# New durations in a kernel's own list schedule, an add moved ahead of a scaling, and a later row for a second recurrence

## The chip, the cores and the metric

The kernel runs on one core of a Trainium2 chip. The metric is the device time of one execution in microseconds (us), as the median of several runs; lower is better. A core has five engines that each work through their own instructions in order and wait for each other through semaphores: TensorE (PE: matmuls and transposes, results in PSUM), VectorE (DVE), ScalarE (ACT), GpSimd (POOL) and SyncE (SP), which here only issues DMAs. PSUM has eight banks of 512 floats a row. All data is float32; a float32 matmul stands in the trace as two passes.

## The reference

The input `x` has 2 sequences of 4096 tokens with 256 channels. Two sublayers are applied, each on a layer-normed input with a residual around it.

The first is a recurrence over all tokens, channel by channel:

```
r, k, v = three projections of mixes of a token and the one before it
out_t = (exp(b-p)*a + exp(k_t+u-p)*v_t) / (exp(b-p) + exp(k_t+u-p) + eps)
a, b  = a decayed running sum of exp(k)*v, and the log of that of exp(k)
y     = group_norm(sigmoid(r) * out) @ W_o.T
```

The second has two layers, each an attention over windows of 128 tokens that also sees the window before, and a gated feed-forward part:

```
h = shift_token(x);  q, k, v = split(h @ wqkv)          # 8 heads of 64
q, k = rotary(l2norm(q) * qs), rotary(l2norm(k) * ksc)
x = x + softmax(8 q k^T, masked to i-128 <= j <= i) v @ wo
h = layer_norm(shift_token(x)) @ w1 + b1;  a, g = split(h)
x = x + (a * gelu(g)) @ w2 + b2                          # 682 hidden channels
```

## The kernel before

**Tiling.** Tokens are taken in groups of 128, one window each: 2 sequences x 2 layers x 32 windows are 128 groups, numbered `n` from 0 to 127. Four groups make a block of 512 tokens, `k`. Blocks 0 to 7 are sequence 0 in layer 0, blocks 8 to 15 sequence 0 in layer 1, and blocks 16 to 31 the same for sequence 1. The recurrence of sequence 0 (`rec`, pieces of 512 tokens) runs first, that of sequence 1 (`rec2`, 16 pieces of 256 tokens) beside the attention and feed-forward work of sequence 0. Its tiles lie in one buffer, `arena`, so the profile names its work `arena` (the first one also borrows `hm`, `x`, `qk`, `sq`, `hT` and others).

**A group's attention.** For group `n`, `transpose_qk` turns queries and keys, `scores` makes the scores of eight heads in four PSUM banks, in one piece with the products of group `n-1`'s probabilities with its values (`values`). `softmax(n, g)`, g from 0 to 3, handles two heads of one bank: `copy_predicated` packs the two windows' scores into the 129 columns that a query can see, a minimum over them gives the shift `nmx`, ScalarE takes the exponentials into `pr` with their sums in `sums`, VectorE the reciprocal, and `scaled` multiplies `pr` by it. Column 0 of `pr` holds the weight of the last token of the window before, column 1 that of the first token of the own window; each later column holds a token of one of the two windows. `transpose_p(n, s)`, s = 0 or 1, takes four heads (g = 0, 1 or g = 2, 3): it adds column 0 of `pr` to column 1 (lines 1102 to 1104), then transposes columns 1 to 128 on TensorE; the value products take these with the own values `vt`, and a masked copy `pB`, into which the transposed column 0 goes as row 0, with `dv`, the older values less the own. The sum of columns 0 and 1 is what makes the two products add up to both weights. A group that opens a sequence (`lone(n)`) has no window before it and needs no add.

**What sets the order.** The program isn't issued as it is written. `Plan` (line 174) records every operation with what it depends on, and a row (`plan.at`, mostly `n`). `cost` (line 294) gives each operation a `step`, after which its engine is free for the next, and a `time`, after which its result is there, from constants of its kind and its number of elements. `order` (line 361) then walks a list schedule: on each engine it takes the operation that can start first, and among those that can start within 1 ns of it the one of the smallest row:

```
for s, g in cands:
    if s <= t0 + 1:
        key = g[0].at
        if best is None or key < best[0]:
            best = (key, s, g)
```

Operations marked "either" (copies, and the scalings `scaled`) go to whichever of VectorE and ScalarE could start them first. `lock` marks operations of VectorE and GpSimd that are taken not to overlap; `TURN` is what TensorE is taken to lose between matmuls of full size and those of half the rows or columns. PSUM banks are handed out in the same walk. `give` (line 487) emits the operations in order of their planned starts. On the chip, each engine follows that order and waits where the plan was wrong. All emitted instructions stand in the profile under the lines of `give`: L503, with L497 and L499 for `scaled` on VectorE and ScalarE.

**The second recurrence.** In the loop over `n` (line 1359 on), piece `c` of `rec2` is recorded at row `n + 0.5` of the group with `int(c * R_SLOTS / rec2.n) == n`, R_SLOTS being 54: its scans, and ahead of them load, norm, transposes and projections of piece `c + 1`. Rows only rank operations that are ready together.

Of the kernel before, what the change touches and what calls it, by code (L numbers as in the profile page):

```python
# [30 lines left out]
LN_EPS = 1e-5  # L31
NEG = -1e38
MASKED = -3e38
R_SLOTS = 54
AHEAD = 1

ARENA = (
# [18 lines left out]

SEM = 60
LOAD = 1283
TURN = {"row": 195, "col": 95, "full": 95}
SETS = {AF.Exp: 1, AF.Tanh: 1, AF.Gelu: 2, AF.Ln: 3}  # L60
QUADS = 4

# [111 lines left out]
class Plan:  # L174
# [119 lines left out]
    def cost(self, o):  # L294
# [6 lines left out]
        if o.eng == "tensor":  # L301
# [10 lines left out]
                o.step /= 2  # L312
            o.time = o.step + 150
        elif o.eng == "vector":
            if name == "tensor_tensor_reduce":
                d = 210 + 1.05 * n
            elif name == "tensor_tensor_scan":
                d, o.lock = 2.48 * n, True
            elif name in ("scalar_tensor_tensor", "tensor_tensor"):
                d, o.lock = 175 + 1.04 * n, wide > 1  # L320
            elif name in ("tensor_scalar", "tensor_copy") and not psum:
                d, o.lock = 230 + 0.45 * n, n > 64
            elif name == "bn_aggr":
                d = 180
            elif name == "reciprocal":
                d = 165 + 4 * n
            else:
                d = 150 + 1.04 * n
            o.step, o.time = max(d - 70, 60), d
        elif o.eng in ("scalar", "either"):  # L330
            d = 160 + 0.83 * n
            if name == "scaled":
                d = 40 + 1.4 * n
            if name == "activation":
                o.set = SETS.get(o.args[2])
                if "accum_out" in o.kw:
                    d += 320
                elif o.args[2] in (AF.Gelu, AF.Identity):
                    d = 40 + 1.4 * n
            o.step, o.time = d - 100, d  # L340
        elif o.eng == "gpsimd":
            if name == "tensor_tensor":
                d = 600 + 160 * n if ALU.pow in o.args else 150 + 2.25 * n
                o.lock = n > 64
            elif name == "tensor_scalar":
                d = 200 + 1.12 * n
                o.lock = n > 64
            else:
                d = 170 + 0.98 * n
                o.lock = n > 64  # L350
            o.step, o.time = d, d
        else:
            v = min(views, key=lambda v: v.shape[0] * v.idx.size)
            size = 4 * v.shape[0] * v.idx.size
            rows = max(v.shape[0] if v.shape[0] > 1 else v.shape[1] for v in views)
            ways = max(k for k in range(1, 17) if rows % k == 0)
            o.passes = size / 170 if ways == 16 else size / (25 * ways)
            o.step, o.time = 60, 2000 + o.passes


    def order(self):
# [47 lines left out]
        while todo:  # L409
# [23 lines left out]
            for o in g:  # L433
# [73 lines left out]
def kernel(ctx: ExitStack, tc: tile.TileContext, a: dict, out: bass.AP):  # L507
# [547 lines left out]
    def softmax(n, g):  # L1055
# [27 lines left out]
        for m in range(2):  # L1083
# [272 lines left out]
    for n in range(NN + 6):  # L1356
# [152 lines left out]
```

## Time and profile before

| what | us |
|---|---|
| median of 3 runs | 3045.44 |
| lowest and highest of them | 3045.35 and 3046.44 |
| the profiled execution, its own time | 3047.84 |
| its span in the trace | 3046.0 |
| TensorE: matmuls 128x512 with `wqkv` | 728.1 busy, 1536 passes of 598 ns |
| TensorE: matmuls 128x512 with `w1` (`hT`) | 646.7 busy, 1408 passes of 595 ns |
| VectorE: adds of `pr`, 128x4 | 61.5 busy, 248 of 248 ns |
| VectorE: scalings of `pr`, 128x129 (L497) | 84.9 busy, 274 of 336 ns |
| ScalarE: scalings of `pr`, 128x129 (L499) | 260.0 busy, 738 with the 128x128 ones, 398 ns each |
| ScalarE: exponentials into `pr` | 362.4 busy, 1024 of 365 ns |
| ScalarE: loads of its function tables | 146.3 busy, 114 of 1283 ns |

Busy time of an engine is the time in which an instruction of it is in flight; two that follow each other closely overlap. A "releaser" is the instruction whose semaphore ended a wait. The mean granted clock of TensorE is 0.994 of full speed.

### The profile page before, as it was taken

The page shows a single profiled execution, that of the slowest core. Times are in us where ns is not written, and L with a number is a line of the kernel's source. Part 1 is how long each engine was busy: PE and PEld are TensorE (multiplying, and loading weights), DVE is VectorE, ACT ScalarE, POOL GpSimd, SP SyncE. Part 2 cuts the span into 40 slices and gives each one's busy share as a digit, 9 for nine tenths or more (in the row PEclk, how much of TensorE's full clock was granted, in tenths as well). Part 3 has the DMA queues.
Part 4 walks back from the last instruction along what each step waited for, and adds up shares of the span by engine and source line. Part 5 has one row for each costly group of instructions (what it writes and reads, how often), then busy time and mean ns, then how long its engine had stood idle before and what let it go on. Part 6 is the DMA issues. An engine that isn't in the chain of part 4 may idle for free.

```text
span 3046.0 us, 47917 instructions
## 1 busy us (share of the span) xinstructions
PE 2977.8 (98%) x15500; PEld 1932.6 (63%) x15500; DVE 2513.2 (83%) x5487; ACT 1731.2 (57%) x4592; POOL 1434.7 (47%) x1705
## 2 busy tenths in 40 slices
PE   8979999999999999999999999999999999999998
PEld 3456566666666666666666666666666666666665
DVE  7889999989889898887787787878878787877774
ACT  6877665666556666655555455545545555555542
POOL 2227555445444545444455444444444554554541
PEclk9989999999999999999999999999999999999999
DMA  3222112111112121111112211112112111111110
GB/s 96 88 76 89 44 57 63 53 58 51 59 51 80 54 69 54 53 53 56 53 54 82 83 58 60 57 59 60 54 45 66 61 59 56 55 53 51 48 43 23
DMA packets 178163, 181.66 MB, mean 60 GB/s; under 512 B 27028, under 2 KB 147700, under 8 KB 177400
## 3 DMA queue, kind: packets, MB, share of 16 engines
q1 hardware_dynamic: 177912, 178.59, 19.0%
q8 instruction: 123, 2.02, 0.3%
q14 instruction: 128, 1.05, 0.1%
HBM read 78.38 MB, written 33.55 MB: 37 GB/s over the span
## 4 chain that ended last, share of the span: by engine, by line
PE 75%; DVE 13%; ACT 6%; issue 2%; POOL 2%; SPq 1%; DMA 1%; DVEq 0%; POOLq 0%; ACTq 0%
PE bank L503 75%; DVE arena L503 3%; ACT arena L503 2%; DVE sq L503 1%; DVE qk L503 1%; ACT L503 1%; DVE bank L503 1%; SPq L503 1%; DVE nmx L503 1%; DVE x L503 1%; ACT pr L499 1%; DVE pr L497 1%; DMA h<-x 1%; DVE hm L503 1%; POOL rs L503 1%
## 5 line engine op out<-in xcount | busy, mean ns | idle before, releaser
L503 PE MATMUL bank<-wqkv,xT 128*128 128x512 f32 x1536 | 728.1, 598 | 0.0
L503 PE MATMUL bank<-hT,w 128*128 128x512 f32 (+1 forms) x1408 | 646.7, 595 | 0.2 <-DVE hT L503 0.2
L503 POOL TENSOR_TENSOR t<-qk,tab 128x256 f32<-128x256 f32 x512 | 379.8, 762 | 502.5 <-DVE qk L503 293.8
L503 ACT ACTIVATE pr<-bank,nmx 128x129 f32<-128x129 f32 (+1 forms) x1024 | 362.4, 365 | 332.3 <-DVE nmx L503 331.8
L503 PEld LDWEIGHTS bank<-hT,w 128*128 128x128 f32 (+1 forms) x1408 | 257.6, 190 | 273.1 <-issue 256.4
L503 PEld LDWEIGHTS bank<-wqkv,xT 128*128 128x128 f32 x1536 | 269.1, 190 | 240.1 <-issue 230.4
L503 POOL TENSOR_TENSOR rn<-rn,mhalf 128x16 f32<-128x16 f32 x128 | 386.1, 3017 | 10.3
L503 PE MATMUL bank<-w,hm 128*128 128x256 f32 x1536 | 351.8, 379 | 0.0
L503 PEld LDWEIGHTS bank<-w,hm 128*128 128x128 f32 x1536 | 287.1, 190 | 51.1 <-issue 15.3
L499 ACT ACTIVATE pr<-pr,sums 128x129 f32<-128x129 f32 (+1 forms) x738 | 260.0, 398 | 40.6 <-DVE sums L503 38.0
L503 PE MATMUL bank<-kT,qT 64*128 64x256 f32 (+1 forms) x2048 | 252.4, 386 | 0.0
L503 PE MATMUL bank<-wo,oT 128*128 128x256 f32 x1024 | 248.0, 385 | 2.5 <-ACT oT L503 1.7
L503 PEld LDWEIGHTS bank<-wo,oT 128*128 128x128 f32 x1024 | 189.7, 190 | 74.7 <-issue 35.4
L503 DVE TENSOR_TENSOR pB<-bank,backs 128x512 f32<-128x512 f32 x248 | 169.3, 683 | 51.8 <-ACT pT L503 50.0
L503 PEld LDWEIGHTS bank<-kT,qT 64*128 64x128 f32 x2048 | 185.3, 186 | 39.0 <-issue 15.9
L503 PEld LDWEIGHTS bank<-mats,pr 128*128 128x128 f32 (+1 forms) x1148 | 130.8, 135 | 120.2 <-issue 40.3
L503 DVE COPY_PREDICATED bank<-packs,bank 128x254 f32<-128x254 int32 x496 | 186.0, 420 | 25.1 <-PE bank L503 24.9
L503 ACT ACTIVATION_READ_ACCUMULATOR pr<-bank,nmx 128x1 f32 x1024 | 206.7, 202 | 0.0
L503 PE MATMUL bank<-pT,vt 128*64 128x128 f32 x2048 | 203.6, 279 | 0.0
L503 PE MATMUL bank<-mats,pr 128*128 128x128 f32 (+1 forms) x1148 | 173.3, 275 | 22.1 <-DVE pr L503 18.8
L503 PE MATMUL bank<-arena,wold 128*128 128x256 f32 (+1 forms) x600 | 193.7, 447 | 0.4 <-DMA wold<-in_w_rkv_dram 0.4
L503 POOL TENSOR_TENSOR tab<-tab,qks 128x256 f32<-128x256 f32 x128 | 109.6, 857 | 177.2 <-DMA tab<-in_c_rot_dram 167.3
(148 smaller groups left out, 5440.6 us busy)
## 6 DMA issues: line engine op xcount, KB each, us to landing
vr<-vt SPq DMA_DIRECT2D x124, 224.0 KB
tab<-in_c_rot_dram SPq DMA_DIRECT2D x128, 128.0 KB
kT<-kT SPq DMA_DIRECT2D x64, 256.0 KB
z<-zd SPq DMA_DIRECT2D x16, 512.0 KB
x<-in_x_dram SPq DMA_DIRECT2D x16, 512.0 KB
x1d<-x SPq DMA_DIRECT2D x16, 512.0 KB
x<-x1d SPq DMA_DIRECT2D x16, 512.0 KB
h<-x SPq DMA_DIRECT2D x128, 64.0 KB
```

Source lines behind the costliest of these rows:

```text
L497: self.nc.vector.tensor_scalar(dst, src, scale, None, ALU.mult)
L499: self.nc.scalar.activation(dst, src, AF.Copy, scale=scale)
L503: getattr(getattr(self.nc, o.eng), name)(*args, **kw)
```

## The change

It has three parts. First, constants in `cost`, `order` and `TURN`, which say how long operations take: among them a ScalarE scaling of 129 columns goes from 40 + 1.4 x 129 to 305 + 0.76 x 129 ns, an exponential with its sum from 160 + 0.83 x 129 + 320 ns to 160 + 0.83 x 129 + 85 ns of engine time with another 200 ns to its result, a VectorE scaling from 230 + 0.45 x 129 to 155 + 0.98 x 129 ns, and the turn of TensorE to full size from 95 to 199 ns. The tail of a VectorE instruction that may overlap the next goes from 70 to 85 ns. Second, the add of `pr`'s columns 0 and 1 moves from `transpose_p`, after the scaling, to `softmax`, between reciprocal and scaling, where it takes two heads at a time. Third, pieces of `rec2` are recorded five groups later (NW is 4) and closer together (R_SLOTS 50 for 54).

```diff
-R_SLOTS = 54
+R_SLOTS = 50
...
-TURN = {"row": 195, "col": 95, "full": 95}
+TURN = {"row": 195, "col": 95, "full": 199}
...
         elif o.eng == "vector":
+            d = 150 + 1.04 * n
             if name == "tensor_tensor_reduce":
-                d = 210 + 1.05 * n
+                d = 240 + 1.04 * n
             elif name == "tensor_tensor_scan":
-                d, o.lock = 2.48 * n, True
-            elif name in ("scalar_tensor_tensor", "tensor_tensor"):
-                d, o.lock = 175 + 1.04 * n, wide > 1
-            elif name in ("tensor_scalar", "tensor_copy") and not psum:
+                d, o.lock = 203 + 2.1 * n, True
+            elif name == "scalar_tensor_tensor":
+                d, o.lock = 200 + 1.05 * n, wide > 1
+            elif name == "tensor_tensor":
+                o.lock = wide > 1
+            elif name == "tensor_scalar":
+                d, o.lock = 155 + (1.27 if psum else 0.98) * n, not psum and n > 64
+            elif name == "tensor_copy" and not psum:
                 d, o.lock = 230 + 0.45 * n, n > 64
...
-            o.step, o.time = max(d - 70, 60), d
+            o.step, o.time = max(d - 85, 60), d
+        elif o.eng in ("scalar", "either"):
+            d = (160 if psum else 195) + 0.83 * n
+            if name == "scaled":
+                d = 305 + 0.76 * n
+            elif name == "activation":
+                o.set = SETS.get(o.args[2])
+                if o.args[2] == AF.Identity:
+                    d = 365 + 0.87 * n
+                elif isinstance(o.kw.get("bias"), View):
+                    d += 85
+            o.step, o.time = d - 100, d
+            if "accum_out" in o.kw:
+                o.time = d + 200
...
-        elif o.eng in ("scalar", "either"):
-            d = 160 + 0.83 * n
-            if name == "scaled":
-                d = 40 + 1.4 * n
-            if name == "activation":
-                o.set = SETS.get(o.args[2])
-                if "accum_out" in o.kw:
-                    d += 320
-                elif o.args[2] in (AF.Gelu, AF.Identity):
-                    d = 40 + 1.4 * n
-            o.step, o.time = d - 100, d
...
-                    time = 150 + 1.04 * n if o.name == "copy" else 230 + 0.45 * n
-                    step = time - 70
+                    time = 150 + 1.04 * n if o.name == "copy" else 155 + 0.98 * n
+                    step = time - 85
...
         nc.vector.reciprocal(sums, sums)
+        if not lone(n):
...
+            p0 = prs[n][:, h0 : h0 + 3 : 2, :]
+            nc.vector.tensor_tensor(p0[:, :, 1], p0[:, :, 1], p0[:, :, 0], ALU.add)
         for m in range(2):
             ph = prs[n][:, h0 + 2 * m, off:]
             nc.either.scaled(ph, ph, sums[:, m : m + 1])
...
         pr = prs[n]
-        if not lone(n):
-            p0 = pr[:, 4 * s : 4 * s + 4, 1]
-            nc.vector.tensor_tensor(p0, p0, pr[:, 4 * s : 4 * s + 4, 0], ALU.add)
         ppt = bank([P, 4, W])
...
         for c in range(rec2.n):
-            if int(c * R_SLOTS / rec2.n) == n:
+            if NW + 1 + int(c * R_SLOTS / rec2.n) == n:
                 plan.at(n + 0.5)
```

GpSimd's constants change in the same way, by up to 30% (its power function on one element from 760 to 586 ns).

More of the change, by code (lines that the diff above doesn't have):

```diff
@@ L322, in cost @@
                 d, o.lock = 230 + 0.45 * n, n > 64
             elif name == "bn_aggr":
-                d = 180
+                d = 172
             elif name == "reciprocal":
-                d = 165 + 4 * n
-            else:
-                d = 150 + 1.04 * n
-            o.step, o.time = max(d - 70, 60), d
-        elif o.eng in ("scalar", "either"):
-            d = 160 + 0.83 * n
-            if name == "scaled":
-                d = 40 + 1.4 * n
-            if name == "activation":
-                o.set = SETS.get(o.args[2])
-                if "accum_out" in o.kw:
-                    d += 320
-                elif o.args[2] in (AF.Gelu, AF.Identity):
-                    d = 40 + 1.4 * n
-            o.step, o.time = d - 100, d
[L341 to L350, printed above, removed]
+                d = 147 + 4 * n
@@ new lines, in cost @@
+            o.step, o.time = max(d - 85, 60), d
[12 more added lines that the diff above has]
+                o.time = d + 200
+        elif o.eng == "gpsimd":
+            o.lock = n > 64
+            if name == "tensor_tensor":
+                d = 430 + 156 * n if ALU.pow in o.args else 140 + 2.22 * n
+            elif name == "tensor_scalar":
+                d = 230 + 1.12 * n
+            else:
+                d = (100 if name == "memset" else 187) + 0.98 * n
```

## The prediction

> **What bounds the kernel now.** I read the page's busy shares and chain first, then the windows by stage, then TensorE's waits, then one late transpose in the timeline.
>
> ```profile
> PE 2977.8 (98%) x15500; PEld 1932.6 (63%) x15500; DVE 2513.2 (83%) x5487; ACT 1731.2 (57%) x4592; POOL 1434.7 (47%) x1705
> PE 75%; DVE 13%; ACT 6%; issue 2%; POOL 2%; SPq 1%; DMA 1%; DVEq 0%; POOLq 0%; ACTq 0%
> ```
>
> TensorE is the bound: 3046.0 - 2977.8 = 68.2 us of idle time is nearly all that any order of the same matmuls can give back. The windows (stretch, sum, busy time by engine, granted clock) say where it lies:
>
> ```profile
> 0.00:225.00 225.00, 199.26 (x572) 106.44 (x572) 180.09 (x349) 166.65 (x282) 61.10 (x109) 0.96 0.26 88
> 225.00:375.00 150.00, 138.04 (x732) 90.46 (x732) 139.82 (x332) 100.80 (x266) 98.49 (x120) 0.97 0.21 67
> 375.00:1450.00 1075.00, 1057.79 (x5676) 701.63 (x5674) 950.04 (x2070) 657.06 (x1721) 528.98 (x620) 1.00 0.19 58
> 1450.00:2990.00 1540.00, 1536.15 (x8334) 1003.01 (x8333) 1224.96 (x2700) 797.13 (x2307) 743.10 (x850) 1.00 0.19 58
> 2990.00:3046.00 56.00, 46.52 (x193) 31.10 (x192) 18.26 (x38) 9.54 (x19) 3.02 (x6) 0.93 0.07 23
> ```
>
> Idle TensorE: 25.7 us in the first recurrence, 12.0 while the attention starts, 17.2 while the second recurrence runs beside it, 3.9 afterwards, 9.5 in the tail. VectorE is at 80, 93, 88 and 80% in the first four. Beside idle time there is lost clock: 4% of 225 us is 9 us, 3% of 150 us is 4.5 us, 7% of 56 us is 4 us. By who ended TensorE's waits:
>
> ```profile
> PE bank L503 <- DVE pr L503: 18.8, 27, 2.3
> PE bank L503 <- ACT arena L503: 16.4, 6, 6.5
> PE bank L503 <- DVE h L503: 5.6, 1, 5.6
> PE bank L503 <- DVE qk L503: 4.6, 8, 1.4
> ```
>
> The largest is the transposes of the probabilities `pr`, waiting for VectorE. The timeline around the longest (start, duration, engine, what, idle before):
>
> ```profile
> 762.77 1.20 DVE L503 TENSOR_TENSOR sq<-sq,t 128x1024 f32<-128x1024 f32 x1
> ...
> 762.89 0.70 ACT L499 ACTIVATE pr<-pr,sums 128x129 f32<-128x129 f32 x2
> ...
> 763.89 0.15 DVE L503 RECIPROCAL sums<-sums 128x2 f32<-128x2 f32 x1
> 763.96 0.14 DVE L503 TENSOR_TENSOR pr<-pr 128x4 f32<-128x4 f32 x1
> ...
> 764.15 0.66 PE L503 MATMUL bank<-mats,pr 128*128 128x128 f32 x4 [2.28 <-DVE pr L503]
> ```
>
> The scaling on ScalarE is done at 763.59. The add of four numbers a row then stands behind a 1.20 us product and a reciprocal on VectorE and starts at 763.96. Of the 2.28 us wait, 764.15 - 763.59 = 0.56 us belongs to the add and its queue, the rest to the softmax before it.
>
> **What the Trainium skill says.** "Perfetto Trace Analysis", Identifying the Most-Contended Engine, warns that busy time of matmuls is a bad measure of distance to the limit. The trace agrees: a 128x512 matmul is shown as 598 ns, but four in a row that start at 1609.69 are followed by the next start at 1611.41, 430 ns each. So I count idle time and clock, not the 98%. "TensorE: Matmul & The Clock Gate", HAM oscillation, says that idle gaps of about a window (3.4 us) drop the clock. Here 10 us after the 2.28 us gap the clock is 0.83 (window 762 to 772), and 0.71 in 300 to 310: long gaps cost twice. "Perfetto Trace Analysis", Optimizing Scalar/DVE Operations, puts the fixed cost of a VectorE instruction on SBUF at about 60 ns, with twice that in the profile; the reciprocal above has 150 ns and its successor starts 70 ns after it. "SBUF — State Buffer", in its text on the port pair that VectorE and GpSimd share, calls it an exclusive lock; the add of four numbers has a mean of 248 ns against a median of 161 and a maximum of 696, which fits it standing behind GpSimd at times.
>
> **The change part by part.** The orders of both programs' instructions, engine by engine, show the same work on TensorE (9158 matmul instructions in both), GpSimd and SyncE. VectorE goes from 5489 to 5940, ScalarE from 3570 to 3366.
>
> *The add ahead of the scaling.* One add of four heads after it becomes two adds of two heads, right after the reciprocal, before it. The chain exponentials, reciprocal, scaling, add, transposes loses its last link. Four late transposes in the timeline give what the link costs: 0.56 us (764.15), 1.7 (303.45, from scaling done at 301.70), 0.26 (1067.80) and 0.25 (2479.34). The median is about 0.4; 27 waits make 11 us, with 2 us of clock regained after the longest: -13 us. The ends: -5 (27 x 0.2) and -25 (the whole 18.8 and 6 of clock). The scaling now waits for the add too, 0.07 to 0.15 us later; where both scalings of a pair are late that is taken off again, inside the ends. What is late next is the scaling itself.
>
> *Load moved to VectorE.* Counted from the orders: adds 248 to 496; scalings on VectorE 286 to 506 (ScalarE 738 to 518), since the new costs make a ScalarE scaling about 400 instead of 220 ns; copies out of PSUM on VectorE 628 to 610. With means of one: 248 x 248 ns = 61.5 us, 220 x 336 ns = 73.9, -18 x 680 ns = -12.2, together 123; each of the 451 more instructions overlaps its predecessor by about 60 ns, so about 97 us of busy time. ScalarE loses 220 x 398 ns = 87.6 us, gains 18 copies of 585 ns: about -78. VectorE goes from 83 to 86%. TensorE idles 17.2 us per 1075 us where VectorE is at 88%, and 3.9 per 1540 where it is at 80%: 16.0 against 2.5 per 1000 us over 9 points, 1.5 a point. Groups 5 to 50 gain about 25 us of VectorE work, 2.4 points of that stretch: +4 us. The last 1540 us gain about 58 us, 3.8 points, at half that slope: +4. Together +8 us, between +2 (TensorE always has other work) and +30 (a third of the added work reaches the path).
>
> *The second recurrence five groups later.* Its row only decides between operations that can start at the same time (within 1 ns); what is ready on an idle engine is taken whatever its row. The orders bear this out: ahead of the first softmax the changed program already has 18 of the recurrence's mixing instructions on VectorE, the old one 14; over groups 0 to 4 it has 4 fewer. So it is little "later"; it yields to the first five groups. 12 us of idle and 4.5 of clock are at stake there, with VectorE at 93%. I take -5 us; the ends are 0 and -12. It then runs closer, one piece per 50/16 = 3.1 groups instead of 3.4, and ends one group later (51 for 50); its two following consumers, group 59's loads and group 60's mixing, are far off. I leave that in the +8.
>
> *The new durations in the first 225 us.* The 16.4 us in 6 waits for ScalarE's `arena`, with 9 us of clock, come from the recurrence's serial chain through VectorE, ScalarE and table loads. The new order does more transposes of `arena` ahead and puts eight more copies of it on VectorE (13 to 21 before the first softmax), which is at 80% here. This goes either way: -3 us, ends -12 and +8. The turn cost of TensorE between tile shapes changes nothing that is issued: values and scores stand in one piece, 128 turns of each kind stay. Tail, loads and other waits: the same, 0, with 3 either side.
>
> Later in the program the better-known scaling time also helps the placing of the transposes, but the same table now makes a pair of exponentials with its accumulator 252 ns apart, where the trace has 350 (763.48 to 763.82), and the order on TensorE puts the first transposes on average 5.5 us of matmuls behind the scores in groups 5 to 50, where it was 6.4. Less margin, with a real chain of about 4 us: I take -2 for the whole of it, ends -8 and +8.
>
> Sum: -13 + 8 - 5 - 3 - 2 = -15 us. Against the profiled execution's own 3047.84 us (its span of 3046.0 and 1.84 around it) that is 3033; the median of the runs shown is 2.4 below that execution, so the forecast is 3030 us, -0.5%.
>
> **Rivals.** (A) Most of the stalls go: the pr waits whole with their clock (-25), the start (-12), half of the first recurrence's waits and clock (-12), no price for VectorE's load: about 2997. For it: all these waits are short, and other matmuls are ready nearly everywhere. Against: the first recurrence is a serial chain, and VectorE gets fuller. (B) Nothing changes: the waits for "DVE pr" turn into waits for the scaling (ACT pr), and -8 meets +8: 3045. For it: in 764.15 only 0.56 of 2.28 us was the add's. (C) Slower: VectorE becomes the bound between 375 and 1450 us. It is at 88% there and 93% in the 150 us before; with some 25 to 35 us added it has under 100 us of free time left in 1075, and in-order queues lose some of it. If a third of its added 97 us comes through, and the smaller margin of the transposes costs 8, less 18 for add and start, it is 3045 + 32 + 8 - 18 = 3067. It decides once TensorE's idle time in that stretch rises from 17 to over 40 us. Against it: the same list of costs knows VectorE's time better than before.
>
> **How the numbers follow.** Forecast 0.51, A 0.19, B 0.14, C 0.16. About 0.2% (6 us) is what a measurement can tell here, so faster means below 3039, slower above 3051.5. Faster: A, and nearly all of the forecast's own spread, 0.70; same 0.14; slower 0.16. The forecast's own ends are 3012 and 3042; the range takes in most of A and half of C: 2999 to 3054.
>
> **What would show it.** Right: "DVE pr" gone or below 6 us in TensorE's waits with "ACT pr" and the VectorE scaling below 10; TensorE idle between 225 and 375 us below 9; VectorE's busy time near 2610 us and ScalarE's near 1655; TensorE idle 375 to 1450 between 10 and 20. Wrong: TensorE's waits for the scaling above 20 us (the add hid nothing), VectorE over 95% from 375 to 1450 with TensorE's idle time above 40 (C), or the first 225 us longer or shorter by more than 10.

## The result and the profile after

The change made the kernel slower: 3058.66 us (median of 6 runs, 3054.87 to 3060.43) against 3047.01 for the kernel before in the same session (6 runs, 3045.35 to 3051.85). The ratio is 1.0035, its 95% interval 1.0022 to 1.0048. The profiled executions took 3059.6 and 3047.84 us, with spans of 3057.8 and 3046.0. The prediction was 3030.

The busy shares and the chain, from the page of the changed kernel:

```profile
PE 2985.6 (98%) x15500; PEld 1935.4 (63%) x15500; DVE 2581.5 (84%) x5938; ACT 1643.9 (54%) x4388; POOL 1451.9 (47%) x1705
PE 70%; DVE 16%; ACT 7%; issue 2%; POOL 2%; DMA 2%; SPq 1%; DVEq 0%; ACTq 0%; POOLq 0%
```

VectorE gained 68 us of busy time and ScalarE lost 87: the load moved about as forecast. In the chain TensorE's share falls from 75 to 70%: more of the time is set by what TensorE waits for. The windows of the changed kernel, by the same stages (stretch, its length, busy time of PE, PEld, DVE, ACT and POOL, granted clock, DMA share, GB/s):

```profile
0.00:225.00 225.00, 203.05 (x589) 110.78 (x590) 192.02 (x370) 162.18 (x272) 63.70 (x110) 0.96 0.27 88
225.00:375.00 150.00, 138.31 (x738) 89.92 (x737) 143.15 (x359) 99.93 (x261) 98.92 (x123) 0.99 0.23 70
375.00:1450.00 1075.00, 1048.79 (x5620) 696.54 (x5619) 959.41 (x2192) 623.67 (x1646) 520.78 (x611) 0.99 0.19 57
1450.00:2990.00 1540.00, 1535.12 (x8284) 998.66 (x8282) 1258.54 (x2960) 743.25 (x2176) 763.05 (x853) 1.00 0.19 58
```

TensorE's idle time was 25.7, 12.0, 17.2 and 3.9 us in these stages; it is now 22.0, 11.7, 26.2 and 4.9. The stretch in which the second recurrence runs beside the attention has lost 9 us, at 89% of VectorE's time (959.41 of 1075) where it was 88%.

The windows cut at times, so they don't compare the same work. To do that, each trace is put at the moments at which the scores of a group begin. Group 4's begin at 323.4 us for 329.3 before: 6 us gained in the start, as much as the prediction gave to the later rows (that they are not shown to be the reason is said below). Group 36's begin 10.6 us earlier, but group 40's 3.0 us later; a part of such a difference is only work that stands in another order. At group 52, when the second recurrence is done, the changed kernel is 7.7 us behind, at group 60 it is 10.0, at the end 11.8. So nearly everything is lost between groups 5 and 60, the last 1460 us add 2. Then the waits of TensorE in the changed kernel (line, whose result, us in total, times, longest):

```profile
PE bank L506 <- ACT arena L506: 18.3, 10, 6.1
PE bank L506 <- ACT pr L502: 16.5, 22, 4.1
PE bank L506 <- DVE qk L506: 5.8, 8, 1.8
PE bank L506 <- DVE pr L500: 5.4, 8, 1.4
PE bank L506 <- DVE gmv L506: 4.3, 1, 4.3
```

Lines 500 and 502 are `scaled` on VectorE and ScalarE, line 506 is everything else. The wait for the add (DVE pr, 18.8 us in 27) is gone from the list. In its place stands the wait for the scaling, 16.5 and 5.4 us. All waits for `pr`, the add's and the scalings' together, were 21.7 us and are 21.9.

This list counts only idle time that shows after the modelled end of a matmul. A 128x128 matmul is shown as 275 ns, where in a row they start 109 ns apart, so shorter delays hide in TensorE's busy time; that rose by 7.8 of the 11.8 us. So the delay is counted a second way: from the start of the TensorE instruction ahead of a transpose of `pr` to the transpose's own start, less the median of that time after an instruction of the same shape in all twenty traces, summed over the 1148 passes. By this count, called "late" below, the transposes of `pr` are 32.2 us late before and 37.7 after: somewhat later, though the chain ahead of them has a link less. The rest of the loss is spread; 5 us of it stand ahead of the value products. The worst place, in the timeline (start, duration, engine, what, idle time before it):

```profile
650.12 2.71 DVE L506 TENSOR_TENSOR_SCAN arena<-arena 128x256 f32<-128x256 f32 x2
...
652.86 0.69 DVE L506 TENSOR_TENSOR arena<-arena 128x512 f32<-128x512 f32 x1
...
653.47 1.21 DVE L506 TENSOR_REDUCE rn<-sq 128x16 f32<-128x1024 f32 x1
...
654.60 0.74 DVE L506 COPY_PREDICATED bank<-packs,bank 128x254 f32<-128x254 int32 x2
...
655.75 1.28 ACT L506 ACT_TABLE_LOAD   x1 [5.58 <-DVE nmx L506]
...
658.43 0.38 ACT L506 ACTIVATE pr<-bank,nmx 128x129 f32<-128x129 f32 x1
...
658.77 0.42 ACT L502 ACTIVATE pr<-pr,sums 128x129 f32<-128x129 f32 x1
...
659.25 0.48 PE L506 MATMUL bank<-mats,pr 128*128 128x128 f32 x1 [4.15 <-ACT pr L502]
```

The scores of this group began at 649.46. VectorE packs them only at 654.60, because two scans, a product and a reduction stand in its queue first; ScalarE then loads its table, and the fifth exponential (658.43) stands ahead of the scaling for which TensorE has been waiting. The list schedule put this transpose where it thought the softmax would be over. The windows around it show a second cost:

```profile
650.00:655.00 5.00, 5.00 (x26) 3.16 (x22) 4.93 (x7) 0.16 (x1) 2.51 (x4) 1.00 0.15 46
655.00:660.00 5.00, 0.69 (x3) 0.30 (x3) 3.87 (x18) 4.24 (x17) 3.05 (x3) 0.88 0.04 11
660.00:665.00 5.00, 5.00 (x9) 2.42 (x10) 4.47 (x9) 2.58 (x9) 0.00 (x0) 0.50 0.20 48
```

From 660 to 665 TensorE has half its clock, and 128x512 matmuls start 853 ns apart, for 429 later on: 2.5 us in this window on top of the 4.15. This agrees with what the Trainium skill says in "TensorE: Matmul & The Clock Gate", HAM oscillation, of idle gaps of about a window. Over the whole program it makes no difference: the mean granted clock is 0.994 in both kernels.

So two readings stand against each other. Either VectorE's load makes the chain late (the prediction's +8 was too small), or the transposes stand too early, because the new durations make the list believe in a short softmax (the prediction's -2).

### The profile page after: what moved, and what is told of

The parts are those of the page before. It is cut to its first block, busy times and chain, and to the rows that moved or that the text cites. A ratio compares the mean times of both kernels' runs of the same rounds, so it can differ in the third digit from the quotient of the medians.

```text
span 3057.8 us, 48471 instructions
## 1 busy us (share of the span) xinstructions
PE 2985.6 (98%) x15500; PEld 1935.4 (63%) x15500; DVE 2581.5 (84%) x5938; ACT 1643.9 (54%) x4388; POOL 1451.9 (47%) x1705
## 4 chain that ended last, share of the span: by engine, by line
PE 70%; DVE 16%; ACT 7%; issue 2%; POOL 2%; DMA 2%; SPq 1%; DVEq 0%; ACTq 0%; POOLq 0%
PE bank L506 70%; DVE arena L506 4%; ACT pr L506 2%; DVE sq L506 2%; ACT arena L506 1%; DVE pB L506 1%; ACT L506 1%; POOL rs L506 1%; DVE bank L506 1%; DVE qk L506 1%; SPq L506 1%; ACT pr L502 1%; DMA h<-x 1%; DVE pr L500 1%; DVE x L506 1%
## 5 line engine op out<-in xcount | busy, mean ns | idle before, releaser
L506 PE MATMUL bank<-wqkv,xT 128*128 128x512 f32 x1536 | 735.5, 602 | 0.0
L506 ACT ACTIVATE pr<-bank,nmx 128x129 f32<-128x129 f32 (+1 forms) x1024 | 371.0, 379 | 409.6 <-DVE nmx L506 409.2
L506 PEld LDWEIGHTS bank<-w,hm 128*128 128x128 f32 x1536 | 287.8, 190 | 56.1 <-issue 17.2
L502 ACT ACTIVATE pr<-pr,sums 128x129 f32<-128x129 f32 (+1 forms) x518 | 192.2, 413 | 61.7 <-DVE pr L506 58.5
L506 ACT ACTIVATION_READ_ACCUMULATOR pr<-bank,nmx 128x1 f32 x1024 | 220.2, 215 | 0.0
L506 PEld LDWEIGHTS bank<-mats,pr 128*128 128x128 f32 x1148 | 132.8, 135 | 132.2 <-ACT pr L502 48.0
L506 PE MATMUL bank<-mats,pr 128*128 128x128 f32 x1148 | 177.9, 276 | 24.7 <-ACT pr L502 16.5
L506 PE MATMUL bank<-pB,dv 128*64 128x128 f32 x1984 | 194.1, 273 | 3.8 <-DMA pB<-last 3.8
L506 DVE TENSOR_REDUCE nmx<-bank 128x2 f32<-128x258 f32 x496 | 194.5, 418 | 0.0
```

What stands on the lines that cost most here:

```text
L502: self.nc.scalar.activation(dst, src, AF.Copy, scale=scale)
L506: getattr(getattr(self.nc, o.eng), name)(*args, **kw)
```

## The yardstick for the second reading

One number per kernel orders the runs below: what the list schedule takes for four exponentials and four scalings one after the other on ScalarE, from one start to the next. It comes from the constants in `cost`, for 129 columns; it is no time of the chip, and since some scalings go to VectorE it only ranks the kernels. Each term is a `step`: the duration less the 100 ns by which the list lets ScalarE instructions overlap, so the 352 ns of the new exponential hold its engine for 252. Before: 4 x (487 + 121) = 2.43 us. After: 4 x (252 + 303) = 2.22 us. The chip, in the timeline of the kernel before:

```profile
664.22 0.36 ACT L503 ACTIVATE pr<-bank,nmx 128x129 f32<-128x129 f32 x1
664.56 0.37 ACT L503 ACTIVATE pr<-bank,nmx 128x129 f32<-128x129 f32 x1
664.90 0.37 ACT L503 ACTIVATE pr<-bank,nmx 128x129 f32<-128x129 f32 x1
...
668.01 1.33 ACT L499 ACTIVATE pr<-pr,sums 128x129 f32<-128x129 f32 x4
```

340 ns from one exponential to the next, 333 per scaling: 4 x (340 + 333) = 2.7 us. The old list had the exponential 40% too long and the scaling at a third of what it takes, and the two errors nearly cancelled. The new list has the scaling right (303) and the exponential too short (252): it leaves out the read of the accumulator, which in the trace stands on ScalarE between each two of them. The sum moved further from the truth.

## The experiments

The expectations name four theories. Load: VectorE's added work makes the chain late. Margin: the list's softmax is too short, so the transposes stand too early. Scatter: any other order of the same work moves the time by some us, and nothing more is behind it. Rows: the second recurrence, begun later, crowds the groups up to 51. Kernels that ran together share their runs of the kernel before (3046 to 3047 us each time). First the table; "list" is the yardstick, "waits" all of TensorE's waits for `pr` in the profiled execution, "late" the second count of their delay given above.

| run | what it is | add | list, us | median, us | ratio to before, 95% | waits, us | late, us | VectorE busy, us |
|---|---|---|---|---|---|---|---|---|
| before | | behind | 2.43 | 3047.0 | | 21.7 | 32.2 | 2513 |
| e8 | before, semaphore 61 ns | behind | 2.43 | 3053.1 | 1.0023 (1.0013 to 1.0034) | 22.0 | 32.3 | 2505 |
| e3 | rows alone | behind | 2.43 | 3042.5 | 0.9986 (0.9979 to 0.9993) | 21.8 | 32.4 | 2513 |
| e7 | before, exponential 352 | behind | 1.89 | 3080.7 | 1.0118 (1.0102 to 1.0133) | 40.5 | 63.4 | 2536 |
| e1 | durations alone | behind | 2.22 | 3079.6 | 1.0109 (1.0092 to 1.0126) | 36.9 | 64.8 | 2600 |
| e11 | after, exponential 352, old add | behind | 2.62 | 3058.0 | 1.0037 (1.0024 to 1.0050) | 27.3 | 41.1 | 2570 |
| e18 | e11 and 300 ns of margin | behind | 2.62 + | 3063.5 | 1.0058 (1.0043 to 1.0073) | 31.3 | 45.1 | 2569 |
| e2 | add alone | ahead | 2.43 | 3050.5 | 1.0014 (1.0007 to 1.0021) | 20.8 | 29.2 | 2543 |
| e4 | add and rows | ahead | 2.43 | 3052.1 | 1.0017 (1.0009 to 1.0025) | 20.1 | 28.0 | 2542 |
| e6 | after, old scaling times | ahead | 1.49 | 3067.7 | 1.0074 (1.0059 to 1.0089) | 29.7 | 44.9 | 2550 |
| after | | ahead | 2.22 | 3058.7 | 1.0035 (1.0022 to 1.0048) | 21.9 | 37.7 | 2582 |
| e13 | after, semaphore 61 ns | ahead | 2.22 | 3057.6 | 1.0032 (1.0019 to 1.0044) | 26.5 | 42.7 | 2586 |
| e14 | after and 400 ns of margin | ahead | 2.22 + | 3049.8 | 1.0009 (1.0002 to 1.0016) | 18.5 | 31.2 | 2581 |
| e5 | after, exponential 352 | ahead | 2.62 | 3043.9 | 0.9992 (0.9983 to 1.0000) | 20.4 | 29.1 | 2627 |
| e16 | e5, semaphore 61 ns | ahead | 2.62 | 3038.6 | 0.9976 (0.9968 to 0.9984) | 16.0 | 23.6 | 2629 |
| e12 | e5, old rows | ahead | 2.62 | 3048.6 | 1.0004 (0.9995 to 1.0012) | 17.0 | 24.3 | 2623 |
| e9 | after, exponential 487 | ahead | 3.16 | 3052.1 | 1.0017 (1.0010 to 1.0024) | 25.1 | 35.0 | 2606 |
| e10 | after, exponential 600 | ahead | 3.61 | 3058.5 | 1.0036 (1.0024 to 1.0048) | 20.1 | 31.4 | 2620 |
| e15 | e5 and 300 ns of margin | ahead | 2.62 + | 3034.3 | 0.9964 (0.9951 to 0.9977) | 18.1 | 24.7 | 2620 |
| e17 | e5 and 600 ns of margin | ahead | 2.62 + | 3037.9 | 0.9975 (0.9965 to 0.9985) | 10.7 | 17.8 | 2616 |

### The parts alone

**e1_costs**: the new `cost`, TURN and the times in `order` alone; add and rows as before.

```
         for c in range(rec2.n):
-            if NW + 1 + int(c * R_SLOTS / rec2.n) == n:
+            if int(c * R_SLOTS / rec2.n) == n:
...
     def transpose_p(n, s):
...
+        if not lone(n):
+            p0 = pr[:, 4 * s : 4 * s + 4, 1]
+            nc.vector.tensor_tensor(p0, p0, pr[:, 4 * s : 4 * s + 4, 0], ALU.add)
```

(shown against the changed kernel; R_SLOTS is 54 again too)

> Only the new durations, with the add and the rows of the second recurrence as before. Load theory (the new durations send some 220 scalings to VectorE, which then reaches the softmax late while the second recurrence runs beside it): slower than before by 10 us or more, 3056 to 3070, lost between groups 6 and 50. Scatter theory (any new order of this list schedule lands some us up or down, with no one cause): anywhere within 10 us of 3047. Rows theory (the loss comes from the second recurrence being packed closer): not slower than before, 3035 to 3048.

Measured: 3079.6 us, 33 above the kernel before. TensorE's waits for `pr` in its trace:

```profile
PE bank L506 <- DVE pr L506: 35.8, 30, 3.4
PE bank L506 <- DVE pr L500: 0.7, 1, 0.7
PE bank L506 <- ACT pr L502: 0.4, 2, 0.2
```

The wait for the add has doubled, from 18.8 us in 27 to 35.8 in 30. Of the 32 us between the two traces at their ends, 28 are there by group 52. By the second count the transposes of `pr` are 64.8 us late for 32.2, which is the whole difference. The durations are the whole loss of the change, and more than it. With add and rows on top (the changed kernel) 21 us come back. The load theory's own forecast for this run (3056 to 3070) was too small.

**e2_add**: the add moved ahead of the scaling, nothing else of the change.

```
         nc.vector.reciprocal(sums, sums)
+        if not lone(n):
+            p0 = prs[n][:, h0 : h0 + 3 : 2, :]
+            nc.vector.tensor_tensor(p0[:, :, 1], p0[:, :, 1], p0[:, :, 0], ALU.add)
...
-        if not lone(n):
-            p0 = pr[:, 4 * s : 4 * s + 4, 1]
-            nc.vector.tensor_tensor(p0, p0, pr[:, 4 * s : 4 * s + 4, 0], ALU.add)
```

> Only the add moved ahead of the scaling, costs and rows as before. Load theory and my prediction's term: faster by 5 to 15 us, 3032 to 3042, with TensorE's waits for the add gone. Scatter theory: within 10 us of 3047 either way. Rows theory: faster by 5 to 15, as in the load theory.

Measured: 3050.5 us. TensorE's waits for `pr` in it:

```profile
PE bank L503 <- DVE pr L497: 11.9, 16, 2.0
PE bank L503 <- ACT pr L499: 8.9, 10, 2.4
```

Lines 497 and 499 are the scalings here: 20.8 us for the 21.7 with the add behind. This misses the 3032 to 3042 us that the load theory and the prediction's term had. The list schedule takes the shorter chain into account: in the mean of all groups the transposes stand 7.4 us of TensorE's work behind the start of the scores, for 7.8 before, so they come earlier by about the length of the link, and what is left to wait for is nearly the same.

**e3_rows**: R_SLOTS 50 and the shift by `NW + 1` alone. **e4_add_rows**: this and the add, so the change without its durations.

```
-R_SLOTS = 54
+R_SLOTS = 50
...
-            if int(c * R_SLOTS / rec2.n) == n:
+            if NW + 1 + int(c * R_SLOTS / rec2.n) == n:
```

> Only the rows of the second recurrence: five groups later, 50 slots for 54. Rows theory: slower by 10 us or more, 3056 to 3065, lost between groups 36 and 50. Load theory: 3038 to 3047, gaining up to 7 us over groups 0 to 6. Scatter theory: within 10 us either way.

> The change without its new durations: add and rows. Load theory: the sum of the two gains, 3028 to 3042, so that the durations alone stand for the loss. Rows theory: 3045 to 3060. Scatter theory: not the sum of the two single runs, off from it by 8 us or more.

Measured: 3042.5 and 3052.1 us. Rows alone are 4 us faster than before, with the add 2 us slower than the add alone. Neither is larger than the scatter that e8 shows, so no more than "some us" can be said of them. e4 misses the 3028 to 3042 us of the load theory.

### Load or margin

**e5_after_exp350**: the changed kernel with 352 ns from one exponential with a sum to the next in the list, for 252, and its result there after 462 ns, for 552.

```
             if "accum_out" in o.kw:
-                o.time = d + 200
+                o.step, o.time = d, d + 110
```

> The changed kernel with one duration corrected: an exponential with its sum takes ScalarE 352 ns (the trace has 350 from one to the next) in place of 252, and its result is there after 462 in place of 552. Margin theory (the new table makes the softmax look some 1 us shorter than it is, so that the transposes of the probabilities are put too early on TensorE and wait): back to 3035 to 3048, with TensorE's waits for pr under 12 us from 22. Load theory (the 220 scalings moved to VectorE are the loss): 3055 to 3063, unchanged. Scatter theory: within 10 us of 3058.

Measured: 3043.9 us, 15 below the changed kernel. The busy shares on its page:

```profile
PE 2980.6 (98%) x15500; PEld 1936.7 (64%) x15500; DVE 2626.6 (86%) x5939; ACT 1640.9 (54%) x4388; POOL 1468.2 (48%) x1705
```

VectorE has as many instructions as in the changed kernel (71 scalings fewer, 72 copies more) and is busy 45 us longer, and the kernel is faster: for this step the load theory falls. The waits for `pr` fell only from 21.9 to 20.4 us, where the margin theory wanted less than 12. The second count shows more of it: 29.1 us late for 37.7, 8.6 of the 13.5 us between the two traces.

**e6_after_oldscaled**: the changed kernel with the scaling's old durations, to send the scalings back to ScalarE.

```
             if name == "scaled":
-                d = 305 + 0.76 * n
+                d = 40 + 1.4 * n
...
-                    time = 150 + 1.04 * n if o.name == "copy" else 155 + 0.98 * n
+                    time = 150 + 1.04 * n if o.name == "copy" else 230 + 0.45 * n
```

**e7_before_exp350**: the kernel before with the exponential at 352 ns instead of 487.

```
                 if "accum_out" in o.kw:
-                    d += 320
+                    d += 185
```

**e8_before_sem61**: the control for scatter.

```
-SEM = 60
+SEM = 61
```

> The changed kernel with the old durations of the scaling alone (ScalarE 40 + 1.4 n, VectorE 230 + 0.45 n), which sends most scalings back to ScalarE. Load theory: back to 3040 to 3050, with VectorE's busy time near 2550. Margin theory: slower than the changed kernel, 3060 to 3085, because the softmax then looks shorter still and nothing is left that made up for the exponentials. Scatter theory: within 10 us of 3058.

> The kernel before with one duration corrected: the exponential with its sum takes 352 ns of ScalarE and 452 to its result, for 487 and 587. Margin theory: slower, 3053 to 3080, since the old value was too long by 135 ns each and so made up for the scaling that was too short. Load theory: 3040 to 3050. Scatter theory: within 10 us of 3047.

> The kernel before with the semaphore's delay in the plan at 61 ns for 60: no cause, only another order. It measures the scatter. Scatter theory: 5 to 15 us away from 3047, on either side. Margin and load theory: within 4 us of 3047.

Measured: 3067.7, 3080.7 and 3053.1 us. In e6 only 77 of the 220 scalings went back, so it is a weaker trial than was meant; still VectorE is busy 32 us less than in the changed kernel, and the time is 9 us longer. It has 429 scalings on VectorE and e5 435, and the two are 24 us apart, so their number there does not set the time either. e7 is the telling one: an exponential closer to the truth makes the kernel before 34 us slower, because, as the margin theory has it, the scaling that it had covered is still too short. The transposes stand 7.4 us of work behind the scores for 7.8, and the waits for `pr` double to 40.5 us. e8 says what a difference is worth: one nanosecond in another constant costs 6 us.

### How much margin, and what the other edits are worth with it

**e9_after_exp487** and **e10_after_exp600**: as e5, with 487 and 600 ns. **e11_exp350_noadd**: e5 with the add back behind the scaling. **e12_exp350_norows**: e5 with the rows of before.

```
             if "accum_out" in o.kw:
-                o.time = d + 200
+                o.step, o.time = d + 135, d + 235
```

(d + 248 and d + 348 in e10; the edits of e11 and e12 are e1's halves)

> The changed kernel with an exponential with its sum held for 487 ns from one to the next in the list schedule (what the old list held, the new one 252, the trace shows 350). Margin theory: more margin than with 352 (which gave 3043.9 us), so 3030 to 3044 us, and TensorE's waits for the scalings (both engines) below 20 us. Scatter theory (any other order of the same work moves the time by about 6 us, the margin does nothing): anywhere in 3044 to 3062 us, with waits for the scalings that need not fall. VectorE's load theory: as the changed kernel, 3055 to 3062 us, as VectorE has the same work.

> The changed kernel with an exponential with its sum held for 600 ns. Margin theory: the scalings are over long before TensorE gets to the transposes: waits for the scalings below 12 us; the time is 3030 to 3045 us, unless the longer softmax makes other work late (then the waits for the scalings fall but those of others rise). Scatter theory: 3044 to 3062 us, waits for the scalings not ordered by the margin. Load theory: 3055 to 3062 us.

> The changed kernel with an exponential held for 352 ns and the add of two weights put back behind the scaling (one add of four heads): the price of the add alone where the list's softmax has its measured length. If the add hid a link of the chain as predicted: 8 to 14 us above the 3043.9 of the kernel with 352 ns, 3052 to 3058 us. If the list schedule takes the link into its own account, so that it costs nothing either way: within 6 us of 3043.9.

> The changed kernel with an exponential held for 352 ns and the second recurrence begun where it began before: the price of its later begin. If the later begin is worth 5 us as predicted: 3047 to 3051 us, with TensorE's idle time lost between the start of the attention's first group and the sixth. If it is only another order: within 6 us of 3043.9 to either side.

Measured: 3052.1, 3058.5, 3058.0 and 3048.6 us. The first two miss what margin alone would give: beyond the true duration the time rises again. In e10 the waits for `pr` are 20.1 us and those for `h` (9.1 for 3.1 in the changed kernel), `qk` (7.3 for 5.8) and `oT` (4.3 for 2.5) have grown. In e11 the add behind the scaling costs 14 us, as the prediction's -13 had it; at the old durations it was worth nothing (e2). In e12 the later begin is worth 4.7 us, which is the predicted 5 in size and within the scatter, but not in place: with the later rows (e5) the scores of group 6 begin at 363.7 us, without them (e12) at 358.0.

### Margin without holding an engine

e9 and e10 also held ScalarE longer in the list, which misplaces its other work. So the next runs leave every `step` alone and move only the moment at which a scaling's result counts as there, on both engines. (The list also keeps GpSimd's locked operations off a VectorE scaling until then; what that does by itself was not tried.)

**e13_after_sem61** and **e16_exp350_sem61**: the controls of the changed kernel and of e5, with SEM at 61. **e14_after_margin400**: the changed kernel with 400 ns of margin. **e15_exp350_margin300**: e5 with 300 ns.

```
+            if name == "scaled":
+                o.time = d + 300
             if "accum_out" in o.kw:
-                o.time = d + 200
+                o.step, o.time = d, d + 110
...
                     step = time - 85
+                    time += 300 if o.name == "scaled" else 0
```

> Control for the changed kernel: the list's time for a semaphore 61 instead of 60 ns, which says nothing of the softmax but shuffles the order. Margin theory: the time stays within 6 us of the changed kernel's 3058.7 (3052 to 3064), and TensorE's waits for the scalings stay at 18 us or more. Scatter theory: as likely below 3050 as above.

> The changed kernel with 400 ns (4 exponentials by the 98 ns that the list has them too short) added to the time after which a scaling's result counts as there, with no engine held longer: margin alone. Margin theory: 3038 to 3048 us, like the kernel with the exponential at 352 ns, waits for the scalings below 15 us. Occupation theory (what helped at 352 ns was that the list holds ScalarE as long as it is really held; margin alone does nothing): 3053 to 3062 us. Scatter theory: no order.

> The changed kernel with an exponential at 352 ns and 300 ns more until a scaling's result counts as there: margin beyond the measured durations, with no engine held longer. Margin theory in its strong form (waits for the scalings are what is left to win): 3030 to 3040 us, waits for the scalings below 12 us. If measured durations are already the best point, as 487 and 600 ns for the exponential suggest: 3044 to 3054 us, since other work comes late in their place.

> Control for the kernel with the exponential at 352 ns: 61 instead of 60 ns for a semaphore. Margin theory: within 6 us of 3043.9 (3038 to 3050). Scatter theory: the 15 us between this kernel and the changed one are luck of the order, so this one is as likely to stand near 3058 as near 3044.

Measured: 3057.6, 3049.8, 3034.3 and 3038.6 us. The two controls stay within 6 us of their kernels, so the 15 us between the changed kernel and e5 are more than another order moved here. Margin alone regains 9 of them (e14, a little less than expected, with waits of 18.5 us where less than 15 were). On top of the true duration it makes a version that beats both kernels: e15, 0.36% below the kernel before and 0.8% below the changed one (3034.3 / 3058.7). How much of that is the margin's is less sure: e15 is 9.6 us below e5, but only 4.3 below e5's control e16. Its busy shares and its waits for `pr`:

```profile
PE 2972.7 (98%) x15500; PEld 1936.4 (64%) x15500; DVE 2620.1 (86%) x5931; ACT 1642.8 (54%) x4396; POOL 1467.2 (48%) x1705
```

```profile
PE bank L509 <- DVE pr L503: 9.2, 13, 1.9
PE bank L509 <- ACT pr L505: 8.5, 7, 3.0
```

Lines 503 and 505 are the scalings. They are 20 of the 22 waits for `pr` (30 in the changed kernel), and with the last two 18.1 us: fewer, though not below the 12 us that the strong form of the margin theory wanted.

**e17_exp350_margin600**: 600 ns for 300. **e18_margin300_noadd**: e15 with the add behind the scaling.

```
             if name == "scaled":
-                o.time = d + 300
+                o.time = d + 600
...
-                    time += 300 if o.name == "scaled" else 0
+                    time += 600 if o.name == "scaled" else 0
```

> The changed kernel with an exponential at 352 ns and 600 ns more until a scaling's result counts as there (300 ns gave 3034.3 us). Margin theory: waits for the scalings fall on below the 17.7 us of 300 ns; the time is 3028 to 3040 us, where other work does not come late in their place. If 300 ns was a lucky order: 3040 to 3050 us, about where the two kernels with 352 ns and no margin stand (3043.9, 3038.6).

> The kernel with 352 ns and 300 ns of margin, with the add put back behind the scaling: what the add ahead is worth where TensorE has margin. If the chain of the softmax is what counts, as at 352 ns without margin (14 us): 3044 to 3050 us. If margin takes its place (the add, 0.25 us, is done within the 0.3 us): within 6 us of 3034.3.

Measured: 3037.9 and 3063.5 us. The waits for `pr` and `qk` in e17:

```profile
PE bank L509 <- DVE qk L509: 8.3, 13, 1.4
...
PE bank L509 <- DVE pr L503: 5.6, 12, 1.1
PE bank L509 <- ACT pr L505: 4.6, 5, 2.8
```

0, 300 and 600 ns of margin leave 20.4, 18.1 and 10.7 us of waits for `pr`. That 600 ns lower them is clear; at 300 ns they are no lower than in e16, which has no margin and 16.0. With 600 ns others take their place, `qk` with 8.3 us for 4.1 in e15, and in time the two margins and e16 are within 4.3 us, which is scatter. e18 missed both of its expectations. A margin on the scaling delays the add's place in VectorE's queue as well, and the transposes follow the add with no margin at all:

```profile
PE bank L509 <- DVE pr L509: 31.3, 48, 2.0
```

With the scaling's result late in the list, the add is queued on VectorE behind more work. So margin would help only on the operation on which TensorE waits itself. Between e15 and e18 the add's place is worth 29 us. That reading of e18 rests on its waits and on the code; a kernel with the margin on the add itself was not run.

### The runs together

With the add ahead the times follow the yardstick, up to about the chip's own length: 1.49 us in the list gives 3067.7, 2.22 gives 3058, 2.43 gives 3051, 2.62 (nearest to the chip's 2.7) gives 3039 to 3049, and 3.16 and 3.61 give 3052 and 3058 again; margin that holds no engine lowers it to 3034. With the add behind, 1.89 and 2.22 give 3080 and 2.43 gives 3047, but 2.62 gives 3058 (e11), 11 us worse than the kernel before. So the exponential isn't all that is wrong with the new durations under the old add; what else is, these runs don't tell.

"Late" follows the times more closely than "waits" do, with the add in either place: where a kernel is over 15 us slower than before (e1, e6, e7, e18), 12 to 33 us more stand ahead of the transposes of `pr`. That this is where the time goes is shown. How the durations bring it about is shown only in part. The two columns below are means over the 128 groups, from the start of a group's scores: TensorE's work that stands ahead of the first transposes, each instruction at the median start-to-start time of its shape, and when these transposes really start.

| run | work ahead, us | start, us |
|---|---|---|
| before | 7.81 | 8.22 |
| e7 | 7.39 | 7.93 |
| e1 | 7.75 | 8.40 |
| after | 7.29 | 7.77 |
| e5 | 7.27 | 7.70 |
| e15 | 7.33 | 7.75 |

In e7 the transposes stand earlier than before, as the margin theory says. In e1 they stand where they stood and start later, so there it is the softmax that comes later, in the orders that the new durations make; VectorE's scalings take 449 ns in the mean there, for 336 before. Nor does e5 put them later than the changed kernel does. So what counts is how far the real softmax falls behind the list's; whether the transposes move or the softmax does differs from run to run, and for e1 no run separates VectorE's load from the order.

## Why the prediction was wrong

It said 3030 and came out at 3058.7. By its own steps:

- **"Later in the program the better-known scaling time also helps the placing of the transposes ... I take -2 for the whole of it, ends -8 and +8."** This step failed. It saw the wrong duration (the list takes 252 ns where the trace has 350, or 340 by the starts that it names, and the transposes stood 5.5 us behind the scores for 6.4) and priced it at next to nothing. The durations alone cost 33 us (e1), nearly all of it ahead of the transposes of `pr`. In the complete change the exponential's share is 15 us (after against e5, with controls that stay within 6 us). The margin should have been read as the difference of the list's softmax from the true one, before and after: 2.43 and 2.22 us for 2.7. It was read as two corrections of which one helps. That step of the yardstick is small for 33 us, though, and by which route the durations delay the softmax in e1 stays open.
- **The add, -13 ("27 waits make 11 us").** Right in sign and about in size where it counted, beside the new durations: add and rows together take 21 us off e1, the link 14 us in e11 against e5. That the size fits is in part luck. At the old durations, from which the 11 us were read, the link is worth nothing (e2, +3.8 us, within the scatter), where the transposes stand earlier as well (7.4 us of work behind the scores for 7.8). In the changed kernel the wait went from the add to the scaling, 21.9 us for 21.7, which is rival B's mechanism. A wait can't be priced by its length where a list schedule places the waiter. The 68.2 us of idle time were no full measure either, since short delays hide in TensorE's busy time. The mark set for "wrong", waits for the scaling above 20 us, is what came.
- **Load on VectorE, +8.** About 97 us of busy time were forecast and 68 came, since an add of two heads has a mean of 184 ns where 248 were used. What it did by itself is not shown. It isn't what holds the changed kernel back: in e5, e15, e16 and e17 VectorE is busy 34 to 48 us longer, with about as many instructions, and they are 15 to 24 us faster. That speaks against the slope, "1.5 a point", too, which compared two stretches that differ in more than VectorE's load. All these still have over 100 scalings more on VectorE than the kernel before, and for e1 no run takes the load away by itself.
- **The second recurrence five groups later, -5.** Not shown. The changed kernel does gain 6 us by group 4, but the rows alone gain 1.2 there (e3) and the add alone 8.1 (e2), and e5 is 4.4 us behind e12, which lacks the later rows. The price over the whole program (-4.7 from e12 to e5, -4.3 in e3, +1.6 from e2 to e4) is no larger than the scatter.
- **The new durations in the first 225 us, -3.** Nothing: group 0's scores begin at 260.0 us for 259.9.
- **Rival C** said slower, with VectorE as the bound, from 40 us of idle TensorE between 375 and 1450 us. There were 26.2. The sign was its, the mechanism wasn't, apart from its "smaller margin of the transposes costs 8".

What the range lacked: the ends of the terms for the new durations, +8 and +8, came nowhere near the +33 us that they showed by themselves. Why single stalls of several us arise (649 to 659 us above) is not settled further than that VectorE's queue holds recurrence work ahead of the packing of the scores there.

## What to carry to other kernels

Where a list schedule places in-order work, its durations are one system: correcting some of them can uncover an error that another one covered, so compare the planned and the measured length of whole chains, not of instructions, and count what holds the engine until the next start (340 ns here) and not the instruction alone. Margin on the result that the bound engine waits for is better given to the `time` than to the `step`: here 300 and 600 ns in the `time` gave 3034 and 3038 us, and an exponential held for 487 and 600 ns gave 3052 and 3058. Which of the two margins is the better is within the scatter. Idle time after modelled ends shows only a part of what the bound engine loses, so compare its starts too. Before a difference of some us is believed, shuffle the order with a constant that means nothing: here that alone moved the time by 1 to 6 us.

## What was not expected of the hardware

- The same instructions take a little longer in the changed kernel: the exponentials have a mean of 379 ns for 364, the reads of their accumulators 215 for 202, the scalings on ScalarE 413 for 397, one kind of 128x256 scan (`arena` from `arena` alone) 834 for 763. VectorE has more to do beside them; which access holds them up was not taken apart.
- A pair of such scans took 2.71 us from 650.12 on, where the mean of one is 0.83. GpSimd worked on products nearly all the while (1.59 us from 649.62, 1.10 from 651.17). That one slows the other was not tried by itself. The Trainium skill, "SBUF — State Buffer", Who interferes with whom, has a VectorE instruction with two inputs in SBUF contend with a GpSimd one that reads SBUF, the later one waiting until the first is over. The trace fits that in part: the two scans, 1.64 and 1.14 us long, end 0.55 and 0.56 us after the two products, which is less than a whole scan takes.
- After a gap of 4.15 us TensorE had half its clock over the 5 us from 660 on, so the gap cost at least 6.7 us.
